# A graph layer on one core: tiles with their own base and 112 columns, last edges' types found by marks, bias kept in PSUM

## Chip, core and metric

The kernel runs on one core of one Trainium2 chip. The metric is the device time of one execution in microseconds (us). Before the change it is 2237.54 us, the median of three runs (2236.86 to 2239.26). Engines are named as the profile names them: PE (TensorE, matmuls) and PEld (its weight loads), DVE (VectorE), ACT (ScalarE), POOL (GpSimd) and SP (SyncE).

## What is computed

The reference is a residual layer of a relational graph network over 12500 nodes with 256 features, 212500 edges sorted by destination, and 8 edge types. Cut to what matters:

```python
h = jnp.maximum(_layernorm(x, axis=-1), 0.0)
hx = jnp.einsum('ni,rio->rno', h, weight)          # 8 types, 256 x 256 each
msg = hx[edge_type, src]
agg = jax.ops.segment_sum(msg, dst, num_segments=12500)
out = x + agg * 0.5**0.5 + h_bias + (h @ loop_weight) * 0.5**0.5
```

Each node has one edge to itself among its edges, and as the sort is stable and these edges were put behind the others, it is the node's last. Some 16 other edges per node come from random pairs.

## The kernel before

**What is added up.** The kernel does not multiply each message by its type's weights. It sums, for each node and type, the rows `h[src]` of that type's edges, transposed, in a ring `acc` (128 features x 2 halves x 8 types x nodes). When all edges of a group of 128 nodes are in, the group's eight sums are multiplied by the eight weight matrices and added in PSUM.

**Units and tiles.** The edges are cut into 796 units of 267 edges in order of destination (`EDGES`). From each unit the last edges of nodes are taken out, by shifting the other edges forward in a packed row (`sources`, `compacted`), and what is left, at most 256 edges, makes two tiles of 128 edges. There are 1592 tiles. Index work is done for blocks of 128 units at a time, one unit per partition (`prepare`, 7 blocks), some 300 tiles ahead and a few operations per tile (`blocks_ahead`, `background`).

**One tile.** `gather` (line 607) is an indirect DMA on POOL that fetches the 128 rows `h[src]`; while `h` is not yet whole in DRAM (the first 96 tiles) it fetches rows of `x`, which `batch` then normalizes in place. Gathers are issued 58 tiles ahead (`AHEAD`), into buffers for 62. `onehots` (line 620) writes, for four tiles at once on DVE, ones where a column's number equals the edge's column (8 types x a node's place). `edge_sums` (line 647) multiplies the two halves of the gathered rows by this. A float matmul shows as two matmuls and two weight loads in the profile, so a tile has four of each. Both tiles of a unit add into one PSUM bank that holds 22 nodes from the unit's base (`WIN`): the first reaches all 22 (176 columns), the second 18 from the fourth on (144 columns, `REACH`). `add_sums` (line 659) then adds these 2 x 8 x 22 sums into the ring on DVE, at an offset that is read from memory into a register (`load_offsets`, sixteen units at a time). The banks for sums are four (`ps_e`), and the add of a unit is issued one unit later (`LAG`).

**One group.** `begin` (lines 671 to 679) transposes the group's own rows of `h` on PE, copies them on ACT, and writes them on DVE into the ring eight times, each time where the node's last edge has that type: this counts the last edges without gathering them. The types come from `find_types` (lines 686 to 706), once for four groups, in the `finish` of the fourth: for each block that holds some of these nodes (34 pairs in all), DVE writes `places` (line 698), ones where a node is the first of a unit, and 22 matmuls of 512 columns each (line 701) spread the types of a unit's first, second, ... last edge to all partitions. `group_work` multiplies the complete sums: for each group a matmul of `one` and `bias_in` (line 752), and 2 x 9 products of sums and weights (line 758). They are dealt out between the following tiles by a budget, and PE's order is thus written out by hand, as is every engine's (`manual_schedule`). `finish` (line 767) adds the product to `x`, three tiles after it is issued (`REST`), and begins the group six further on.

**Order and end.** `Plan` gives for each group the last unit that can touch it (`last`), from a line below which no base lies. A node outside a tile's reach would be counted by `verdict`, and the program's second path (`general_path`) would then run behind the first. On these inputs it does not run.

Of the kernel before, what the change touches and what calls it, by code (L numbers as in the profile page):

```python
# [28 lines left out]
EDGES = 267  # L29


WIN = 22
REACH = ((0, 22), (4, 18))
# [7 lines left out]
AHEAD = 58  # L41

# [25 lines left out]
class Plan:  # L68
# [6 lines left out]
    def __init__(self, N, E):  # L75
        U = EDGES
        self.NU = NU = -(-E // U)
        self.NT = NU * PAIR - (1 if E - (NU - 1) * U <= P else 0)
        slack = 6.5 * (E / 4) ** 0.5 / U + 1.0
        self.rate = rate = E / (N * U)  # L80

        self.low = [(1 / rate, -slack / rate), (1.1 / rate, -(1.5 + 0.1 * E / U) / rate)]
        self.high = [(1 / rate, slack / rate)]
        self.starts = list(range(0, N, GROUP))
        self.ends = self.starts[1:] + [N]
        self.NG = len(self.starts)
        self.last = [
            min([NU - 1, *(int((e + 2 - b) / a) + 1 for a, b in self.low)]) for e in self.ends]
        self.last[-1] = NU - 1

        self.begin = lambda u: max(0.0, *(a * u + b for a, b in self.low))
        self.blocks = [
            [b for b in range(-(-NU // P))
             if self.begin(b * P) <= e + 2
             and self.high[0][0] * min(NU - 1, b * P + P - 1) + self.high[0][1] + 2 * WIN + 2 >= s]
            for s, e in zip(self.starts[::XG], self.starts[XG::XG] + [N])]
        a, b = self.high[0]
        self.first = [max(0, int((s - WIN - 2 - b) / a) - 1) if s else 0 for s in self.starts]

# [101 lines left out]
def kernel(  # L201
# [16 lines left out]
    C = R * max(n for _, n in REACH)  # L218
    assert KC * R * WIN <= 512
# [8 lines left out]
    TB, SB = (R - 1).bit_length(), (WIN - 1).bit_length()  # L228
# [12 lines left out]
    bias_in = const.tile([1, D], F32, name="bias_in")  # L241
    one = const.tile([1, P], F32, name="one")
    w = const.tile([P, KC, R * D], F32, name="w")
    wl = const.tile([P, KC, D], F32, name="wl")
    low = const.tile([P, NB], F32, name="low")
    high = const.tile([P, NB], F32, name="high")
    counts = const.tile([P, NB], F32, name="counts")
    line = const.tile([P, XG * GROUP + WIN - 1], F32, name="line")
# [9 lines left out]
    with ExitStack() as main:  # L258
# [12 lines left out]
        selves = main.enter_context(tc.tile_pool(name="selves", bufs=SLOTS + 1))  # L271
        types = main.enter_context(tc.tile_pool(name="types", bufs=2))
# [8 lines left out]
        ps_o = main.enter_context(tc.tile_pool(name="ps_o", bufs=2, space=PSUM))  # L281
        msg, oh, offsets, kind = {}, {}, {}, {}
        firsts, loops, typed, gidx, col = {}, {}, {}, {}, {}
# [94 lines left out]
        def last_edges(b, got):  # L378
# [24 lines left out]
            def number():  # L403
                got["ends"] = small.tile([P, 1], F32, name="ends")
                nc.vector.tensor_reduce(got["ends"], got["end"], AX.X, ALU.add)

            def kept():
                nc.vector.tensor_single_scalar(
                    work_tile(got, "kinds", 6, I32)[:, :WIN], packed[:, :WIN], 2 * R - 1,
                    op=ALU.bitwise_and)  # L410
                loops[b] = small.tile([P, WIN], BF16, name="loops")
                nc.vector.scalar_tensor_tensor(
                    loops[b], line[:, :WIN], got["ends"], got["kinds"][:, :WIN],
                    op0=ALU.is_lt, op1=ALU.mult)

            return [selves_, ends, moves, codes, packs, number,
                    *compacted(got, TB + 1, (EDGES - 1).bit_length()), kept]

        def columns(b, got):


            halves = [(slice(i * P, (i + 1) * P), o, n) for i, (o, n) in enumerate(REACH)]

            def bases():
                got["base"] = small.tile([P, 1], F32, name="base")
                nc.vector.tensor_scalar(
                    got["base"], firsts[b], low[:, b : b + 1], high[:, b : b + 1],
                    op0=ALU.max, op1=ALU.min)

            def offs():  # L430
                got["off"] = small.tile([P, 1], F32, name="off")
                nc.vector.tensor_tensor(got["off"], firsts[b], got["base"], op=ALU.subtract)
                got["add"] = small.tile([P, PAIR], F32, name="add")
                for i, (_, o, _) in enumerate(halves):
                    nc.vector.tensor_scalar(
                        got["add"][:, i : i + 1], got["off"], float(R), float(1 - R * o),
                        op0=ALU.mult, op1=ALU.add)
# [15 lines left out]
            def moved():  # L453
                work_tile(got, "col", 2)
                for i, (h, _, _) in enumerate(halves):
# [4 lines left out]
            def to():  # L460
                for h, _, n in halves:
                    nc.vector.scalar_tensor_tensor(
                        got["there"][:, h], got["col"][:, h], float(n * R), got["there"][:, h],
                        op0=ALU.is_le, op1=ALU.mult)
# [13 lines left out]
            def all_():  # L478
                nc.vector.scalar_tensor_tensor(
                    got["valid"], got["ends"], float(WIN), got["valid"], op0=ALU.min, op1=ALU.add)  # L480
# [3 lines left out]
            return [bases, offs, fits, number, there, moved, to, final, valid, sum_, all_,  # L484
                    *turned(got, "col", lambda: col.setdefault(b, cols.tile([P, U], F32, name="cols")))]

        def places(b, got):

            def wraps_():
                got["wrapped"] = small.tile([P, NK], F32, name="wrapped")  # L490
                nc.vector.tensor_scalar(
                    got["wrapped"], wraps, got["base"][:, 0:1], None, op0=ALU.is_lt)

            def turns():
                got["turns"] = small.tile([P, 1], F32, name="turns")
                nc.vector.tensor_reduce(got["turns"], got["wrapped"], AX.X, ALU.add)

            def position():
                got["pos"] = small.tile([P, 1], F32, name="pos")
                nc.vector.scalar_tensor_tensor(  # L500
                    got["pos"], got["turns"], float(-RING), got["base"][:, 0:1],
                    op0=ALU.mult, op1=ALU.add)

            def turn():
                pt = ps_d.tile([P, 512], F32, tag="pt", name="ptr")
                nc.tensor.transpose(pt[0:1, :P], got["pos"], ident)
                place[b] = small.tile([1, P], I32, name="offs")
                nc.vector.tensor_copy(place[b], pt[0:1, :P])
# [119 lines left out]
        def load_offsets(u0):  # L628
            n = min(REGS, NU - u0)
            b, q = divmod(u0, P)  # L630
# [3 lines left out]
            for i, v in enumerate(vals):  # L634
                offsets[u0 + i] = v

        def edge_sums(t):
            m, o = msg.pop(t), oh.pop(t)
            if t % PAIR == 0:
                bank = ps_e.tile([P, 512], F32, name="ps")  # L640
                sums["ps"] = bank[:, : KC * R * WIN].rearrange("p (c k) -> p c k", c=KC)
            ps = sums["ps"]
            i = t % PAIR
            from_, width = (a * R for a in REACH[i])
            end = t == NT - 1 or i == PAIR - 1
            for c in range(KC):
                nc.tensor.matmul(  # L647
                    ps[:, c, from_ : from_ + width], m[:, c * P : (c + 1) * P], o[:, :width],
                    start=(i == 0 and c == 0), stop=(end and c == KC - 1))
# [5 lines left out]
        def add_sums(u, ps):  # L655
            a = acc[:, :, :, bass.ds(offsets.pop(u), WIN)]
# [3 lines left out]
            added[u] = i.ins  # L660

            assert all(g in begun for g in range(plan.NG) if plan.first[g] <= u)
# [22 lines left out]

        def find_types(q):

            if XG * q >= plan.NG:
                return
            while any(b not in loops for b in plan.blocks[q]):  # L690
                background.pop(0)[1]()
            d0 = plan.starts[XG * q]
            n = min(N - d0, XG * GROUP)
            bs = plan.blocks[q]
            pt = ps_d.tile([P, 512], F32, tag="pt", name="ptt")
            for b in bs:
                o = types.tile([P, XG * GROUP + WIN - 1], BF16, name="places")
                nc.vector.tensor_scalar(  # L698
                    o, line, firsts[b], float(WIN - 1 - d0), op0=ALU.subtract, op1=ALU.is_equal)
                for k in range(WIN):  # L700
                    nc.tensor.matmul(  # L701
                        pt[:, :n], loops[b][:, k : k + 1].to_broadcast([P, P]),
                        o[:, WIN - 1 - k : WIN - 1 - k + n],
                        start=(b == bs[0] and k == 0), stop=(b == bs[-1] and k == WIN - 1))
            typed[q] = types.tile([P, XG * GROUP], BF16, name="types")
            nc.scalar.activation(typed[q][:, :n], pt[:, :n], AF.Copy)  # L706
# [36 lines left out]
        def group_work(g):  # L743
# [5 lines left out]
            def product(r, c):  # L749
                if (r, c) == (R, 0):  # L750
                    got["out", g] = ps_o.tile([P, D], F32, name="po")
                    nc.tensor.matmul(  # L752
                        got["out", g][:n], one[:, :n], bias_in, start=True, stop=False)
                if r == R:
                    lhs, rhs = got["self", g][:, c, :n], wl[:, c, :]
                else:
                    lhs, rhs = acc[:, c, r, s0 : s0 + n], w[:, c, r * D : (r + 1) * D]
                i = nc.tensor.matmul(got["out", g][:n], lhs, rhs, start=False,  # L758
                                     stop=(r == R - 1 and c == KC - 1))
                if r < R and first_dep[0]:  # L760
# [3 lines left out]
            def finish():  # L764
                q, k = divmod(g, XG)
                rows_ = got["x", q]
                nc.vector.tensor_add(rows_[:n, k, :], rows_[:n, k, :], got["out", g][:n])  # L767
# [9 lines left out]
                if b % XG == XG - 1:  # L777
                    find_types(b // XG + 1)
# [13 lines left out]
        with tc.manual_schedule():  # L792
# [6 lines left out]
            iota_i = ohs.tile([P, XG * GROUP + WIN - 1], I32, tag="oh", name="iota_i")  # L799
            nc.gpsimd.iota(iota_i, pattern=[[1, XG * GROUP + WIN - 1]], base=0, channel_multiplier=0)  # L800
            tid = small.tile([P, NB], I32, name="tid")
            nc.gpsimd.iota(tid, pattern=[[P, NB]], base=0, channel_multiplier=1)
# [4 lines left out]
            nc.vector.memset(one, 1.0)  # L807
# [182 lines left out]
```

## Time and profile before

| | |
|---|---|
| median of the three runs | 2237.54 us |
| profiled execution: its time, its span | 2238.67 us, 2236.7 us |
| PE busy | 1984.4 us, 89% of the span |
| DVE busy | 1290.3 us, 58% |
| POOL busy | 1512.0 us, 68% |
| ACT busy | 170.4 us, 8% |
| mean granted PE clock | 0.94 of full speed |
| edge matmuls (line 647), products (line 758) | 1103.7 us, 981.9 us in both of its groups |
| matmuls for types (line 701), for the bias (line 752) | 210.7 us, 68.6 us |
| gathers (line 607) | 1592, together 1509.7 us |

The span runs from the first to the last instruction on the chip, and the profiled execution's time includes what lies around it. Busy times of matmuls overlap, because each is counted through its way down the array. Rows of the profile read: line, engine, operation, what is written and read, shape, count, then busy time, mean ns of one, and the idle time just before them with what ended it. Rows of the timeline begin with the start and the length in us; a count `x4` means that consecutive instructions of one kind were joined.

### The profile page before, as it was taken

Reading aid. Unit: us, or ns where it says so; the run is one execution under the profiler, and the core shown is the slowest. Engines: PE = TensorE matmul, PEld = TensorE weight load, DVE = VectorE, ACT = ScalarE, POOL = GpSimd, SP = SyncE. Lnnn points to the kernel's source line nnn. Section 1 sums busy time; section 2 is a strip of 40 time slices with the busy share of each in tenths; the row PEclk is TensorE's granted clock in tenths of the full one; section 3 lists DMA queues with packets and bytes.
Section 4 is the critical chain, followed back from the end, with each engine's and each line's share of the span. In section 5 each row is a group of like instructions: output and inputs, shape, how many; then the busy total and the mean of one; then the engine's idle time right before and its main releaser. Section 6 shows DMA issues by size and latency. Waiting matters only on the chain.

```text
span 2236.7 us, 30467 instructions
## 1 busy us (share of the span) xinstructions
PE 1984.4 (89%) x11073; PEld 1699.8 (76%) x11073; DVE 1290.3 (58%) x3124; ACT 170.4 (8%) x373; POOL 1512.0 (68%) x1618
## 2 busy tenths in 40 slices
PE   2236899999999999999999999999999799999999
PEld 1235788787787787797787797787797687897897
DVE  6787754485464485454584454684455475564552
ACT  1465300000000000000000000000000000000000
POOL 6624677676777677776777776777777576777730
PEclk9556999999999999999999999999999899999999
DMA  4785344343344344344343443444344343443420
GB/s 133 227 277 183 90 132 135 96 133 117 110 133 132 99 134 121 113 133 118 114 134 108 125 134 103 135 133 119 115 135 120 94 130 96 134 133 101 129 68 14
DMA packets 145685, 279.14 MB, mean 125 GB/s; under 512 B 27909, under 2 KB 94590, under 8 KB 145534
## 3 DMA queue, kind: packets, MB, share of 16 engines
q0 software_dynamic: 76416, 208.77, 32.3%
q1 hardware_dynamic: 69118, 68.40, 9.6%
q8 instruction: 90, 1.47, 0.3%
q14 instruction: 61, 0.50, 0.1%
HBM read 251.46 MB, written 25.60 MB: 124 GB/s over the span
## 4 chain that ended last, share of the span: by engine, by line
PE 78%; DVE 13%; issue 3%; ACT 2%; POOL 1%; DMA 1%; DVEq 0%; SPq 0%; ACTq 0%; POOLq 0%
PE ps L647 34%; PE po L758 31%; PE ptt L701 9%; DVE acc L679 4%; PE po L752 2%; DVE oh L620 1%; POOL msg L607 1%; DVE acc L659 1%; DVE moves L331 1%; PE pst L671 1%; DVE fixed L332 1%; DVE e_stats L555 1%; DVE n_stats L555 1%; ACT xt L567 1%; ACT self_t L674 0%
## 5 line engine op out<-in xcount | busy, mean ns | idle before, releaser
L607 POOL DMA_INDIRECT msg<-h,gidx x1496 | 1417.4, 947 | 544.8 <-issue 405.9
L647 PE MATMUL ps<-oh,msg 128*128 128x176 f32 (+1 forms) x6368 | 1103.7, 305 | 79.9 <-ACT msg L567 51.7
L647 PEld LDWEIGHTS ps<-oh,msg 128*128 128x128 f32 x6368 | 1028.6, 194 | 154.3 <-ACT msg L567 54.8
L758 PE MATMUL po<-w,acc 128*128 128x256 f32 x3136 | 870.2, 380 | 0.8 <-DVE flag L521 0.8
L620 DVE TENSOR_TENSOR oh<-fixed,cols 128x704 f32<-128x704 f32 x398 | 353.3, 888 | 445.4 <-PE ps L647 439.9
L659 DVE TENSOR_TENSOR acc<-acc,ps 128x352 f32 x796 | 409.3, 514 | 285.4 <-PE ps L647 278.9
L758 PEld LDWEIGHTS po<-w,acc 128*128 128x128 f32 x3136 | 531.8, 190 | 22.8 <-issue 1.0
L679 DVE SCALAR_TENSOR_TENSOR acc<-types,pst 128x256 f32<-128x256 bf16 (+1 forms) x784 | 267.5, 413 | 113.7 <-ACT self_t L674 113.7
L701 PE MATMUL ptt<-places,loops 128*128 128x512 bf16 (+1 forms) x748 | 210.7, 452 | 95.6 <-DVE places L698 94.9
L701 PEld LDWEIGHTS <-loops 128*128 128x128 bf16 x748 | 83.3, 114 | 217.2 <-DVE places L698 99.1
L674 ACT ACTIVATE self_t<-pst 128x256 f32<-128x256 f32 x98 | 37.4, 382 | 1578.5 <-PE pst L671 1578.5
L607 POOL DMA_INDIRECT msg<-in_x_dram,gidx x96 | 92.3, 962 | 94.7 <-issue 60.7
L758 PE MATMUL po<-wl,self_t 128*128 128x256 f32 x392 | 111.7, 408 | 0.0
L758 PEld LDWEIGHTS po<-wl,self_t 128*128 128x128 f32 x392 | 66.7, 190 | 38.2 <-issue 32.9
L752 PE MATMUL po<-bias_in,one 1*128 1x256 f32 x196 | 68.6, 429 | 0.9 <-DVE xr L767 0.9
L567 ACT ACTIVATE xt<-xt,n_shift,n_rstd 128x256 f32<-128x256 f32 x98 | 51.0, 589 | 29.8 <-DVE n_shift L564 29.8
L567 ACT ACTIVATE msg<-msg,e_shift,e_rstd 128x256 f32<-128x256 f32 x96 | 49.8, 589 | 13.4 <-DVE e_shift L564 13.4
L752 PEld LDWEIGHTS po<-bias_in,one 1*128 1x128 f32 x196 | 28.9, 184 | 23.3 <-issue 21.4
L767 DVE TENSOR_TENSOR xr<-xr,po 128x256 f32<-128x256 f32 x98 | 40.3, 412 | 9.1 <-PE po L758 8.7
L331 DVE TENSOR_SCALAR moves<-fixed 128x267 int32<-128x267 int32 x98 | 42.3, 431 | 2.1
L332 DVE COPY_PREDICATED fixed<-moves,fixed 128x266 int32<-128x266 int32 (+6 forms) x98 | 39.3, 401 | 3.4
L706 ACT ACTIVATE types<-ptt 128x512 bf16<-128x512 f32 (+1 forms) x25 | 14.7, 587 | 322.7 <-PE ptt L701 322.7
(92 smaller groups left out, 327.5 us busy)
## 6 DMA issues: line engine op xcount, KB each, us to landing
msg<-h,gidx POOLq DMA_INDIRECT x1496, 2.8
xt<-in_x_dram SPq DMA_DIRECT2D x24, 512.0 KB, 6.2
h<-xt SPq DMA_DIRECT2D x24, 512.0 KB, 3.8
xr<-in_x_dram SPq DMA_DIRECT2D x24, 512.0 KB, 7.7
out_dram<-xr SPq DMA_DIRECT2D x24, 512.0 KB, 3.6
hr<-h SPq DMA_DIRECT2D x23, 512.0 KB, 5.2
w<-in_L_gnn_weight_dram SPq DMA_DIRECT2D x2, 1024.0 KB, 5.9
msg<-in_x_dram,gidx POOLq DMA_INDIRECT x96, 2.9
```

The lines of the kernel that those rows point to most:

```text
L331: nc.vector.tensor_single_scalar(m, packed, 1 << (bit + k), op=ALU.bitwise_and)
L332: nc.vector.copy_predicated(packed[:, : EDGES - (1 << k)], m[:, 1 << k :], packed[:, 1 << k :])
L555: nc.vector.bn_stats(stats[:n, j, :], rows_[j])
L567: nc.scalar.activation(rows_[j], rows_[j], AF.Relu, bias=shift[:n, j : j + 1], scale=rstd[:n, j : j + 1])
L607: nc.gpsimd.indirect_dma_start(out=msg[t], out_offset=None, in_=table[:, :], in_offset=bass.IndirectOffsetOnAxis(ap=gidx[b][:, at : at + 1 ...
L620: nc.vector.tensor_tensor(o[:, k : k + v, :i, :], iota_f.unsqueeze(1).unsqueeze(1).to_broadcast([P, v, i, C]), of.unsqueeze(3).to_broadcas ...
L647: nc.tensor.matmul(ps[:, c, from_ : from_ + width], m[:, c * P : (c + 1) * P], o[:, :width], start=(i == 0 and c == 0), stop=(end and c == ...
L659: i = nc.vector.tensor_tensor(a, a, ps, op=ALU.add)
L679: i = nc.vector.scalar_tensor_tensor(acc[:, :, r, s0 : s0 + n], of, float(r + 1), pst[:, :, :n], op0=ALU.is_equal, op1=ALU.mult)
L701: nc.tensor.matmul(pt[:, :n], loops[b][:, k : k + 1].to_broadcast([P, P]), o[:, WIN - 1 - k : WIN - 1 - k + n], start=(b == bs[0] and k == ...
L752: nc.tensor.matmul(got["out", g][:n], one[:, :n], bias_in, start=True, stop=False)
L758: i = nc.tensor.matmul(got["out", g][:n], lhs, rhs, start=False, stop=(r == R - 1 and c == KC - 1))
```

## The change

Three things are changed together.

1. Each tile has its own base, its own 14 nodes (112 columns) and its own add into the ring. The base of a unit's second tile is the node of its 129th remaining edge. Both tiles' sums lie beside each other in one bank. Adds, offsets, `Plan.last` and `Plan.first` count tiles instead of units.
2. Types of last edges: per block and per four groups DVE writes two rows of marks over the 512 nodes, one from each unit's first node on and one from its end on (`mark`, one group earlier than the rest). Products of 24 columns of these marks with the unit's 22 types and its first node, and with the same numbers negated, give each node, on its own partition, its unit's types and first node. DVE picks the node's own type, ACT writes it on a diagonal, and one matmul of 512 columns with ones spreads it to all partitions, three tiles later (`spread_types`).
3. The bias is copied once into the second half of the two output banks, and DVE adds it to `x` in `finish`; the matmul with `one` is gone.

```diff
-WIN = 22
-REACH = ((0, 22), (4, 18))
+LASTS = 22
+WIN = 14
...
         def edge_sums(t):
...
-            ps = sums["ps"]
-            i = t % PAIR
-            from_, width = (a * R for a in REACH[i])
-            end = t == NT - 1 or i == PAIR - 1
+            ps = sums["ps"][:, t % PAIR]
             for c in range(KC):
-                nc.tensor.matmul(
-                    ps[:, c, from_ : from_ + width], m[:, c * P : (c + 1) * P], o[:, :width],
-                    start=(i == 0 and c == 0), stop=(end and c == KC - 1))
+                nc.tensor.matmul(ps[:, c], m[:, c * P : (c + 1) * P], o, start=True, stop=True)
...
+        def mark(q):
...
+                for i, edge in enumerate((firsts[b], stops[b])):
+                    nc.vector.tensor_scalar(
+                        m[:, i, :], line, edge, float(-plan.starts[XG * q]),
+                        op0=ALU.subtract, op1=ALU.is_ge)
...
         def find_types(q):
...
-                for k in range(WIN):
+            parts = [(b, m, i) for b, m in marked.pop(q) for i in range(2)]
+            for g in range(XG):
+                for b, m, i in parts:
                     nc.tensor.matmul(
-                        pt[:, :n], loops[b][:, k : k + 1].to_broadcast([P, P]),
-                        o[:, WIN - 1 - k : WIN - 1 - k + n],
-                        start=(b == bs[0] and k == 0), stop=(b == bs[-1] and k == WIN - 1))
+                        pt[:, g, :], m[:, i, g * GROUP : (g + 1) * GROUP], loops[b][:, i, :],
+                        start=(b, m, i) == parts[0], stop=(b, m, i) == parts[-1])
...
+            nc.vector.tensor_tensor(one, one, pt[:, :, :LASTS], op=ALU.mult)
+            kinds = small.tile([P, XG], F32, name="kinds")
+            nc.vector.tensor_reduce(kinds, one, AX.X, ALU.add)
+            marked[q] = marks.tile([P, XG * GROUP], BF16, name="diagonal")
+            for g in range(XG):
+                nc.scalar.activation(
+                    marked[q][:, g * GROUP : (g + 1) * GROUP], ident, AF.Copy,
+                    scale=kinds[:, g : g + 1])
+
+        def spread_types(q):
+
+            pt = ps_d.tile([P, 512], F32, tag="pt", name="ptt")
+            nc.tensor.matmul(pt, ones_b, marked.pop(q), start=True, stop=True)
             typed[q] = types.tile([P, XG * GROUP], BF16, name="types")
-            nc.scalar.activation(typed[q][:, :n], pt[:, :n], AF.Copy)
+            nc.scalar.activation(typed[q], pt, AF.Copy)
...
             def finish():
                 q, k = divmod(g, XG)
                 rows_ = got["x", q]
+                nc.vector.tensor_add(rows_[:n, k, :], rows_[:n, k, :], outs[g % 2][:n, 1, :])
                 nc.vector.tensor_add(rows_[:n, k, :], rows_[:n, k, :], got["out", g][:n])
...
+                if b % XG == XG - 2 and XG * q < plan.NG:
+                    mark(q)
+                if b % XG == XG - 1 and XG * q < plan.NG:
+                    find_types(q)
+                    done["late"].append((done["tile"] + REST, lambda: spread_types(q)))
...
-                if t % PAIR == PAIR - 1 or t == NT - 1:
-                    waiting.append((t // PAIR, ps))
-                while waiting and (len(waiting) > LAG or t == NT - 1):
-                    u, ps = waiting.pop(0)
-                    add_sums(u, ps)
+                waiting.append((t, ps))
+                while waiting and (
+                        t == NT - 1 or t % PAIR == PAIR - 1 and len(waiting) > LAG * PAIR):
+                    for i in range(min(PAIR, len(waiting))):
+                        u, ps = waiting.pop(0)
+                        add_sums(u, ps)
```

## The prediction

> **What bounds the kernel now.** I read the page's busy shares first, then its groups of part 5, then GpSimd's gathers in windows, the timeline of a steady stretch around 1200 us, the groups kept apart by shape, the list of waits, and the timeline of the end.
>
> ```profile
> PE 1984.4 (89%) x11073; PEld 1699.8 (76%) x11073; DVE 1290.3 (58%) x3124; ACT 170.4 (8%) x373; POOL 1512.0 (68%) x1618
> ```
>
> By these busy times TensorE looks like the bound, and GpSimd (POOL) seems to have a third of its time free. It has not:
>
> ```profile
> 1200.63 0.65 PE L647 MATMUL ps<-oh,msg 128*128 128x144 f32 x4
> ...
> 1201.55 0.76 PE L647 MATMUL ps<-oh,msg 128*128 128x176 f32 x4
> 1201.66 0.95 POOL L607 DMA_INDIRECT msg<-h,gidx  x1 [0.30 <-issue]
> ...
> 1202.92 0.94 POOL L607 DMA_INDIRECT msg<-h,gidx  x1 [0.30 <-issue]
> ...
> 1204.10 1.03 PE L758 MATMUL po<-w,acc 128*128 128x256 f32 x4
> ```
>
> Gathers start 1.25 us apart: 0.95 us of work and 0.30 us of "issue", in which GpSimd waits for nothing that the profile shows. The same 1.25 us stands between the first gathers at 13 us, when nothing holds them. So one gather per tile, 1592 of them, costs 1990 us of a span of 2236.7 us. The windows of line 607 show how near it is:
>
> ```profile
> 0.00:300.00 300.00, 160.58 (x169) 0.74 0.59 182
> 300.00:2153.00 1853.00, 1349.16 (x1424) 0.97 0.41 121
> ```
>
> 169 gathers have started by 300 us, the other 1423 take until 2152.2 us: 1.302 us each. TensorE's tiles go at the same pace (the windows of line 647 count 5848 matmuls, four a tile, from 250 to 2150 us: 1462 tiles, 1.30 us each). TensorE sets it: a gather can run only 58 to 62 tiles ahead, and 103.9 us of GpSimd's waits end with a matmul of line 647. When the gathers stop, TensorE still has 84.5 us of work:
>
> ```profile
> 2222.58 0.65 PE L647 MATMUL ps<-oh,msg 128*128 128x144 f32 x4
> ...
> 2232.80 0.42 DVE L767 TENSOR_TENSOR xr<-xr,po 84x256 f32<-84x256 f32 x1 [8.35 <-PE po L758]
> ```
>
> So TensorE is the bound by only 0.05 us a tile; GpSimd comes next.
>
> **The change, TensorE.** Edge sums: each of a tile's four matmuls gets 112 columns instead of 176 or 144.
>
> ```profile
> L647 PE MATMUL ps<-oh,msg 128*128 128x176 f32 x3184 | 622.9, 319 | 79.9 <-ACT msg L567 51.7 <-DVE n_rstd L563 16.9 <-issue 10.0
> L647 PE MATMUL ps<-oh,msg 128*128 128x144 f32 x3184 | 531.1, 290 | 0.0
> ...
> L758 PEld LDWEIGHTS po<-w,acc 128*128 128x128 f32 x3104 | 526.9, 190 | 20.8 <-issue 1.0
> ...
> L758 PEld LDWEIGHTS po<-w,acc 128*84 128x84 f32 x32 | 4.9, 153 | 2.0
> ```
>
> A duration includes the way through the array, so I take spacings: four 176s in 0.76 us with 319 ns for the last are (760-319)/3 = 147 ns apart, four 144s 120 ns, both 0.83 ns a column. 112 columns would be 93 ns. But a weight load grows by 37 ns for 44 columns (190 against 153), 0.84 ns each, so 128 columns hold it for 108 ns. I take 108, the later of the two (bounds 93 and today's mean 133.5): 6368 x 25.5 ns = 162 us less (0 to 258).
>
> Types of last edges: 748 matmuls go, at (4930-452)/21 = 213 ns (the 22 at 1948.40 us on the chain took 4.93 us): 159 us, and with them the wait before each batch, since the places are written behind a group's eight updates on VectorE:
>
> ```profile
> PE ptt L701 <- DVE places L698: 94.9, 24, 8.5
> ```
>
> In their place each of 25 batches gets about 11 products of 24 columns (68 pairs of block and mark, times 4 groups, over 25), at most 114 ns each (bf16 weight load of line 701), one of 512 columns (0.45 us), and a wait for ScalarE's four diagonals, priced by today's waits between nothing and 3.7 us; I take 1.5. That is 3.2 us x 25 = 80 us (43 to 135). Its marks are written a group earlier, so nothing stands before the small products. Net 174 us less (119 to 211).
>
> Bias: 196 matmuls at 0.69-0.43 = 0.26 us, 51 us less. Together 387 us (170 to 520), 0.24 us a tile: TensorE's own pace falls from 1.30 to 1.06 us (0.97 to 1.19). Even the slow end is under 1.25.
>
> **VectorE.** Two rows give its price per element:
>
> ```profile
> L620 DVE TENSOR_TENSOR oh<-fixed,cols 128x704 f32<-128x704 f32 x398 | 353.3, 888 | 445.4 <-PE ps L647 439.9
> L659 DVE TENSOR_TENSOR acc<-acc,ps 128x352 f32 x796 | 409.3, 514 | 285.4 <-PE ps L647 278.9
> ```
>
> The one-hots have 352 elements more than the adds and take 374 ns more: 1.06 ns each and 140 ns fixed. An add of 224 elements is 378 ns, and there are 1592 for 796: +193 us. A one-hot of 448 is 616 ns: -108. Bias adds 98 x 0.41: +40. Marks 68 x 0.49 against 34 places: +17. Six small operations a batch, some 1.2 us x 25: +30. Fifty more loads of sixteen offsets, 0.64 us of idle behind the one at 1157 us: +32. Longer preparation of 7 blocks, about 2 us each: +14. In all +218 us, 0.14 a tile. From 250 to 2150 us VectorE is busy 1070.6 us, 0.73 a tile; it comes to 0.87, under 1.25 if its waits don't grow. While a block is prepared it is over 1.25 for some 48 tiles, which the 62 tiles of messages cover.
>
> **The sum.** Both are quicker than a gather, so GpSimd stops waiting and TensorE catches up until it waits for messages. From 300 us: 1423 x 1.25 = 1779, so the last gather ends at 2079. The start: TensorE has up to 27 us less to do there (113 tiles), VectorE up to 15 us more, and they alternate: 0 (-27 to +15). Marks beside gathers: 34 places delayed them by about 1.5 us in all (one of 2.12 us at 32 us, one of 1.18 at 318): +3 for twice as many (0 to 34). So 2082. Then the tail: landing 1.9 us (2.8 from issue, 0.95 of it work); products that wait behind the last tiles, since group 96 is complete only four tiles before the end and a tile leaves TensorE some 0.8 us: 6 us (0 to 16); last tile 0.65, its two adds 0.8, the last group's 36 products 8, bias and output adds 0.8, the last store 3.5 as now (2236.7-2233.2). That is 21.6 against 84.5 now, so the span is 2103.6. The profiled execution took 2238.67, 1.97 more than its span, and the median shown, 2237.54, is 1.13 under that: **2105 us**.
>
> **A rule weighed.** Of all rows beside a place marker, gathers show 942 to 964 ns nearly everywhere, and 2117 once. The Trainium skill, "SBUF — State Buffer", section "Who interferes with whom", says that a VectorE instruction in a two-port mode keeps GpSimd fully out of their shared ports for its length, and that this form can enter such a mode: a rule against this change, which has twice as many of them. By it 68 x 0.5 us would be lost and the time be 2136; the row gives 3 us, and I keep the row.
>
> **Rivals.**
> *The pair stays the bound (0.12).* TensorE and VectorE wait for each other tile by tile, and their joint pace stays between 1.27 and 1.31: 300 + 1423 x 1.29 = 2136, and behind the last gather stand some 45 us, half of today's 84.5: 2135 to 2230, 2180 in the middle. For it: VectorE's waits today,
>
> ```profile
> DVE oh L620 <- PE ps L647: 439.9, 262, 13.7
> ...
> DVE acc L659 <- PE ps L647: 278.9, 208, 14.2
> ```
>
> Against it: these are waits for a TensorE that is slow.
> *VectorE becomes the bound, slower (0.08).* Its adds stand in order behind the wait for each tile's sums, and there are now twice as many. If every add kept the 0.35 us that it waits now (278.9/796), that is 279 us more beside 1508 busy and 719 of today's waits: 2506 at the worst, 2367 with half of the extra. It decides from 1.31 us a tile, 0.44 over the 0.87. The gathers' lead and the sums' four banks speak against it.
> *It doesn't do what it says (0.01).* An edge outside the 14 nodes sends the whole run to the general path, thousands of us. On the inputs drawn the widest tile spans 12.
> *The start gains too (0.04).* GpSimd loses 300-13-211 = 76 us before 300 us; if a third goes with the shorter matmuls, 2055 to 2078.
> *Gathers are the bound (0.75).* 2078 to 2135, the forecast.
>
> Range: the forecast's cases from 2076, and the quicker half of the pair's: 2076 to 2165. The rest, 0.19, is left out. A measurement of this kernel tells about 0.2% (4.5 us) from no change: faster 0.90, within it 0.02, slower 0.08.
>
> **What would show it.** Right: gathers 1.25 us apart without a break from 300 us to about 2080; TensorE idle with messages as the releaser; edge matmuls near 108 ns apart; adds near 0.38 us, one-hots near 0.62; no wait of 3.7 us before the types; some 22 us from the last gather to the end. Wrong: gathers still waiting for line 647's matmuls after 400 us, VectorE above 85% busy, a gather's own time above 1 us, or a start later than now by more than 15 us.

## The result and the profile after

The changed kernel takes 2130.33 us (median of 4 runs, 2122.65 to 2131.13) against 2237.20 us for the kernel before, run beside it (4 runs, 2236.08 to 2239.26). The ratio is 0.9514, with a 95% interval of 0.9491 to 0.9537: faster, as predicted, and inside the range, but 25 us above the point of 2105. The profiled execution took 2129.83 us with a span of 2128.1. The last four experiments ran on another chip, on which the kernel before took 2779.33 us; their times can't be set beside the others, and why that chip is slower is not settled.

The busy times, from the page of the kernel after:

```profile
PE 1642.2 (77%) x10433; PEld 1497.1 (70%) x10433; DVE 1475.9 (69%) x4268; ACT 202.5 (10%) x473; POOL 1515.6 (71%) x1619
```

No engine is now above 77%. Read by this row alone, nothing bounds the kernel. The gathers' windows (line 637 of the kernel after; columns: stretch, its length, GpSimd's busy time and count of gathers in it, TensorE's granted clock, share of DMA time, GB/s) show what stands closest to it:

```profile
0.00:300.00 300.00, 160.45 (x168) 0.78 0.59 182
300.00:2100.00 1800.00, 1352.79 (x1424) 0.91 0.42 124
2100.00:2128.20 28.20, 0.00 (x0) 0.97 0.10 31
```

By 300 us 168 gathers have run (before: 169), and the other 1424 end at 2099.1 us: 1.263 us each instead of 1.302. The profiled execution is 108.8 us shorter, and nearly all of that lies in two places. The last gather ends 53 us earlier (2099.1 for 2152.2), and the tail behind it is 29.0 us instead of 84.5, which is 55.5 us less. The start gave nothing.

The groups of the parts that changed, from the page's part 5 (busy and mean of one; then the idle time before them and what ended most of it):

```profile
L637 POOL DMA_INDIRECT msg<-h,gidx x1496 | 1421.1, 950 | 489.6 <-issue 413.9
L674 PE MATMUL ps<-oh,msg 128*128 128x112 f32 x6368 | 961.2, 283 | 272.3 <-issue 96.3
L684 DVE TENSOR_TENSOR acc<-acc,ps 128x224 f32 x1592 | 613.1, 385 | 122.6 <-PE ps L674 77.3
L650 DVE TENSOR_TENSOR oh<-fixed,cols 128x448 f32<-128x448 f32 x398 | 246.8, 620 | 204.5 <-PE ps L674 173.0
```

TensorE now idles 272.3 us ahead of the edge matmuls, and what GpSimd waits for between gathers is mostly the "issue" of 0.30 us again (time in which the profile shows nothing that it waits for). VectorE's waits for TensorE, 439.9 and 278.9 us before, are 173.0 and 77.3: the adds stand closer behind TensorE although there are twice as many.

Three rows of the list of waits are new or were expected to go (engine, what it was about to write and its line, what ended the wait; total, times, longest):

```profile
DVE gidx L326 <- DMA msg<-h,gidx: 101.1, 4, 33.8
PE ptt L731 <- DVE acc L704: 83.6, 23, 7.0
DVE rise L348 <- DMA nat_d<-in_dst_dram: 79.7, 3, 71.2
```

The last one hides the largest loss, a single wait of 71.2 us. The timeline of GpSimd, VectorE and TensorE around 1714 us shows where it comes from:

```profile
1713.26 0.95 POOL L637 DMA_INDIRECT msg<-h,gidx  x1 [0.30 <-issue]
1714.22 0.37 POOL L306 IOTA nat_d<- 128x268 int32 x1
1714.61 0.27 SPq L311 DMA_DIRECT2D nat_d<-in_dst_dram  x1
...
1716.46 0.44 DVE L348 TENSOR_TENSOR rise<-nat_d 128x267 f32<-128x267 int32 x1 [71.17 <-DMA nat_d<-in_dst_dram]
...
1718.64 1.60 PE L674 MATMUL ps<-oh,msg 128*128 128x112 f32 x6 [68.19 <-DVE acc L684]
```

The last block of edges is not full, so its index tile is first filled with padding by an iota on GpSimd (line 306), and only then loaded. The iota takes 0.37 us. But it stands in GpSimd's queue behind all the gathers issued ahead of it, and comes up at 1714.22. VectorE has been waiting for the loaded block since 1645.29, its adds stand behind that wait, and TensorE, without free banks for its sums, stands still for 68.19 us. The releaser that the profile names is the load; the cause is the iota ahead of it, as e4 below shows. The windows of all engines (PE, PEld, DVE, ACT, POOL busy, then the clock) show both halves of the loss:

```profile
1600.00:1700.00 100.00, 46.60 (x283) 41.14 (x281) 30.63 (x81) 0.77 (x2) 75.63 (x81) 0.73 0.41 122
1700.00:1800.00 100.00, 64.43 (x373) 58.39 (x374) 69.25 (x201) 3.41 (x9) 66.60 (x71) 0.76 0.38 109
```

In the first, TensorE is busy for 46.6 us, all but a trace of it before 1650, while the gathers go on (81 instructions of GpSimd in 100 us). In the second the gathers have filled all the message buffers and must wait in turn: 71. Between 1700 and 1800 us their starts lie 13.3 us further apart, in all, than 1.25 us each.

### The profile page after: what moved, and what is told of

It reads as the page before. It is cut to its first block, busy times and chain, and to the rows that moved or that the text cites. A ratio compares the mean times of both kernels' runs of the same rounds, so it can differ in the third digit from the quotient of the medians.

```text
span 2128.1 us, 31245 instructions
## 1 busy us (share of the span) xinstructions
PE 1642.2 (77%) x10433; PEld 1497.1 (70%) x10433; DVE 1475.9 (69%) x4268; ACT 202.5 (10%) x473; POOL 1515.6 (71%) x1619
## 4 chain that ended last, share of the span: by engine, by line
PE 62%; DVE 17%; issue 10%; POOL 4%; DMA 3%; ACT 2%; DVEq 1%; SPq 0%; ACTq 0%; POOLq 0%
PE po L808 33%; PE ps L674 28%; DVE acc L704 5%; POOL msg L637 4%; DVE acc L684 3%; DMA msg<-h,gidx 2%; DVE moves L338 1%; DVE e_stats L585 1%; ACT xt L597 1%; PE pst L696 1%; DVE fixed L339 1%; DVE n_stats L585 1%; DVE oh L650 1%; ACT self_t L699 1%; PE ptt L731 1%
## 5 line engine op out<-in xcount | busy, mean ns | idle before, releaser
L674 PEld LDWEIGHTS ps<-oh,msg 128*128 128x128 f32 x6368 | 960.3, 201 | 372.1 <-issue 179.9
L674 PE MATMUL ps<-oh,msg 128*128 128x112 f32 x6368 | 961.2, 283 | 272.3 <-issue 96.3
L808 PE MATMUL po<-w,acc 128*128 128x256 f32 x3136 | 922.8, 398 | 0.8 <-DVE flag L551 0.8
L684 DVE TENSOR_TENSOR acc<-acc,ps 128x224 f32 x1592 | 613.1, 385 | 122.6 <-PE ps L674 77.3
L650 DVE TENSOR_TENSOR oh<-fixed,cols 128x448 f32<-128x448 f32 x398 | 246.8, 620 | 204.5 <-PE ps L674 173.0
L808 PEld LDWEIGHTS po<-wl,self_t 128*128 128x128 f32 x392 | 75.4, 214 | 7.4
L731 PE MATMUL ptt<-loops,mark 128*128 128x24 bf16 x272 | 11.4, 178 | 85.8 <-DVE acc L704 83.6
L731 PEld LDWEIGHTS <-mark 128*128 128x128 bf16 x272 | 9.0, 100 | 95.2 <-DVE acc L704 89.2
L326 DVE CAST gidx<-ptr 128x256 int32<-128x256 f32 x7 | 2.9, 420 | 103.5 <-DMA msg<-h,gidx 101.1
L696 PE MATMUL pst<-ident,hr 128*128 128x128 f32 (+1 forms) x184 | 35.9, 278 | 35.4 <-DVE gidx L326 33.9
L696 PEld LDWEIGHTS pst<-ident,hr 128*128 128x128 f32 (+1 forms) x184 | 23.6, 151 | 35.8 <-DVE gidx L326 34.0
```

What stands on the lines that cost most here:

```text
L650: nc.vector.tensor_tensor(o[:, k : k + v, :i, :], iota_f.unsqueeze(1).unsqueeze(1).to_broadcast([P, v, i, C]), of.unsqueeze(3).to_broadcas ...
L674: nc.tensor.matmul(ps[:, c], m[:, c * P : (c + 1) * P], o, start=True, stop=True)
L684: i = nc.vector.tensor_tensor(a, a, ps, op=ALU.add)
L696: nc.tensor.transpose(pst[:, c, :n], rows_[:n, c * P : (c + 1) * P], ident[:n, :n])
L731: nc.tensor.matmul(pt[:, g, :], m[:, i, g * GROUP : (g + 1) * GROUP], loops[b][:, i, :], start=(b, m, i) == parts[0], stop=(b, m, i) == pa ...
L808: i = nc.tensor.matmul(got["out", g][:n], lhs, rhs, start=(r == R and c == 0), stop=(r == R - 1 and c == KC - 1))
```

## The experiments

**Theories.** *Gathers:* after the change the gathers' period of 1.25 us is the bound, and the gap to the forecast is the iota's wait. *The pair (rival):* TensorE and VectorE, which hand tiles to each other, are still the bound or close to it, and less work for them gives more time. A second question is which of the three parts (tiles of 112 columns, types, bias) brought the gain.

### One more instruction behind each gather

e1_extra_after and e2_extra_before put a GpSimd memset of one column behind each gather, in the kernel after and in the kernel before:

```diff
+    spare = const.tile([P, 1], F32, name="spare")
...
+            nc.gpsimd.memset(spare, 0.0)
```

> The changed kernel with one more instruction on GpSimd behind each gather, a memset of one column of a tile that nothing reads. Seventeen such memsets took 0.63 us at the start of the kernel before, 37 ns each. Theory (gathers set the pace after the change): every ns that a gather's period grows is paid 1592 times, so at least 1592 x 0.037 = 59 us more, about 2190 us, and the growth is 1592 times the growth of the period that the trace shows. Rival (TensorE and VectorE as a pair set the pace, GpSimd has 29% idle): at most 10 us more, 2130 to 2140.

> The kernel before with the same memset behind each gather. Theory (TensorE set the pace at 1.30 us a tile, a gather's period of 1.25 has 0.05 us to spare): if the period grows by 37 ns nothing is lost, 2237 to 2247 us; if it grows by more than 0.05 us, only what is over is paid, and the loss is some 80 us less than in the changed kernel. Rival (gathers bound the kernel before as well): the same loss as in the changed kernel, 59 us or more.

Measured: 2138.82 us (ratio to the kernel before 0.9569, 0.9546 to 0.9593) and 2237.51 us (1.0014, 1.0001 to 1.0026). The kernel after lost 8.5 us, not the expected 59. GpSimd's timeline in the first shows why:

```profile
599.88 0.95 POOL L638 DMA_INDIRECT msg<-h,gidx  x1 [0.19 <-issue]
600.82 0.12 POOL L641 MEMSET spare<- 128x1 f32 x1
601.13 0.95 POOL L638 DMA_INDIRECT msg<-h,gidx  x1 [0.19 <-issue]
```

The period is still 1.25 us: the memset takes 0.12 us, not the expected 37 ns, out of the gap of 0.30, and 0.19 is left. The 8.5 us come from thirteen intervals of 2.42 us: the last gather ends 15.3 us later (2114.4), and the tail behind it is 23.3 us instead of 29.0. What makes these intervals is not known. The experiment does not tell the theories apart, since the load it was to put on the gathers did not arrive. It shows that the gap has room for another short instruction.

The load was made larger, a memset of 256 columns (e9_long_extra_after, e10_long_extra_before), on the slower chip:

```diff
-    spare = const.tile([P, 1], F32, name="spare")
+    spare = const.tile([P, 256], F32, name="spare")
```

> The changed kernel with a memset of 256 columns behind each gather. The one of a single column took 0.12 us and fitted into the 0.30 us between gathers, so the period stayed 1.25 us. One of 128 columns took 0.21 us at the start of the kernel before, so 256 take some 0.33, and the period grows by 0.03 to 0.22 us. Theory (gathers set the pace): the time grows by 1500 to 1592 times the growth of the period that the trace shows, between 45 and 350 us. Rival (the pair of TensorE and VectorE, at about 1.2 us a tile): nothing is lost up to some 0.05 us.

> The kernel before with the memset of 256 columns behind each gather. Theory (TensorE set the pace at 1.30 us, with 0.05 us to spare): the loss is 0.05 x 1423 = 74 us smaller than that of the changed kernel with the same memset, or smaller still by TensorE's end of 84.5 us that hides behind the slower gathers; both kernels come within 60 us of each other, since both then go at the gathers' pace. Rival (no shared bound): they stay 107 us apart.

```profile
1500.70 0.95 POOL L638 DMA_INDIRECT msg<-h,gidx  x1 [0.17 <-issue]
1501.66 0.33 POOL L641 MEMSET spare<- 128x256 f32 x1
1502.15 0.95 POOL L638 DMA_INDIRECT msg<-h,gidx  x1 [0.17 <-issue]
```

These lines are from e9. Now the period grows, to 1.45 us in 1468 of its intervals: 0.95, 0.33 and 0.17. That is the memset and not the chip: in e12, on the same chip without it, 1267 intervals lie within 5 ns of 1.25 us. The time is 2470.72 us, 340 us above the 2130 of the kernel after on another chip; 1592 x 0.20 is 318. These numbers lie close, but they are no evidence for the gathers as the bound. In e9 TensorE does not catch up with them: from 400 us to the last gather (at 2394.4 us) 31 to 62 messages lie ready whenever it begins a tile, it waits for messages 0.1 us in all, and the tail behind the last gather is 74.8 us. The kernel before with the same memset took 2553.24 us, less than the 2779.33 it takes without it on that chip; why is not known. The two runs with the memset lie 82.5 us apart, between the 60 us at most of the theory and the 107 of the rival. The pair of runs does not settle what the bound is.

### Less work for the pair

e3_96_columns makes the tiles 96 columns wide instead of 112. It leaves VectorE 1394.9 us of work instead of 1475.9, and TensorE shorter matmuls:

```diff
-WIN = 14
+WIN = 12
```

> The changed kernel with 12 nodes (96 columns) for a tile instead of 14, which is as wide as the widest tile of these inputs. Theory (gathers): nothing but a few us at the start and the end, 2118 to 2131 us. Rival (the pair sets the pace): VectorE saves 32 elements an add and 16 columns of a one-hot at 1.06 ns, 0.05 us a tile or 81 us, TensorE up to 0.05 us a tile: 2050 to 2090.

Measured: 2120.87 us (0.9491, 0.9472 to 0.951), 9.5 us quicker than the kernel after, inside what the gathers' theory gives and far above the 2050 to 2090 of the rival. 81 us less for VectorE bring under 10.

e11_half_the_gathers asks the opposite: how quick is the pair when gathers cost half? The second tile of each unit uses the first one's rows, so the sums are not the layer's; the work on them is the same, and half of the gathers are left out (padding and preparation as in e8 below):

```diff
+            if i:
+                msg[t] = msg[t - 1]
+                return
```

> The changed kernel with early padding and preparation 240 ahead, in which only the first tile of each unit is gathered and the second multiplies the same rows again: half of the gathers are left out, all other work stays. It measures the pace of TensorE and VectorE without the gathers' bound. Theory (TensorE at 1.06 us a tile after the change, with a start of 300 us to tile 117 that the gathers hardly set, and 13 us at the end): 300 + 1475 x 1.06 + 13 = 1877 us. Rival (VectorE, with its own waits, is as slow as the gathers): 2060 to 2111.

Measured: 1956.4 us (1953.08 to 1959.59), on the slower chip. GpSimd now waits for TensorE, 932.0 us in all, and TensorE's edge matmuls in the window of its line from 500 to 1500 us give the pair's own pace:

```profile
500.00:1500.00 1000.00, 532.58 (x3616) 537.32 (x3614) 0.94 0.29 84
```

3616 matmuls are 904 tiles: 1.106 us each, with whatever that chip costs included. That is under a gather's 1.25, so the rival falls, as far as the pair goes as quickly beside all gathers as beside half of them, which this run does not show; e8, below, has all of them. The time lies 79 us above the theory's 1877 and 104 below the rival's 2060, so the pair has some 0.14 us a tile to spare, not 0.2 (more, if the chip's stops are in the 1.106).

### The padding made early

e4_pad_early makes the padding once, at the start, and lets VectorE copy it, so that nothing but gathers stands in GpSimd's queue. e8_pad_prep also begins the preparation of a block later, 240 tiles ahead of its use instead of 300:

```diff
-                        nc.gpsimd.iota(
-                            n, pattern=[[2, EDGES + 1]], base=N - 2 * EU, channel_multiplier=0)
+                        nc.vector.tensor_copy(n, pad)
...
+            nc.gpsimd.iota(
+                pad, pattern=[[2, EDGES + 1]], base=N - 2 * EU, channel_multiplier=0)
```

```diff
-PREP = 300
+PREP = 240
```

> The changed kernel, in which the padding of the last block's destinations is counted out by GpSimd at the start, into a tile of its own, and copied by VectorE when the block is prepared; before, GpSimd did it in the middle of the gathers. Theory (the instruction stands in GpSimd's queue behind 58 gathers that are issued ahead but not yet run, so VectorE waits 71 us for it at 1645 us, TensorE stands still and gathers stop for 13 us, and TensorE ends 8 tiles behind): no wait of 71 us, no stop of the gathers, 13 to 20 us less, 2110 to 2118 us. Rival (the messages' buffers cover that wait): 2126 to 2131.

> The changed kernel with the early padding and with a block's preparation begun 240 tiles ahead instead of 300. Theory (at 300 VectorE waits 33 us in three of the blocks for the last gathers of the block two before, whose indices it overwrites, since TensorE has caught up with the gathers; at 240 these gathers are done): the waits of VectorE's index write on gathers (101 us) go, but the gathers never stood still for them, so the time is that with the early padding alone, within 5 us. Rival (these waits are paid in the end): some 30 to 100 us less than with the padding alone.

Measured: 2111.89 us (0.9452, 0.9433 to 0.9472) and 2110.89 us (0.9439, 0.9412 to 0.9466). The iota is what caused the 71 us wait, and that cost the kernel 18 us. The windows of the gathers' line in e4:

```profile
0.00:300.00 300.00, 159.63 (x168) 0.78 0.59 182
300.00:2088.00 1788.00, 1353.61 (x1425) 0.92 0.43 125
2088.00:2111.00 23.00, 0.00 (x0) 0.99 0.13 39
```

The gathers end at 2087.4 us, 11.7 earlier; the tail is 23.0 instead of 29.0. Over 300 us to the end their starts lie only 6.8 us further apart than 1.25 each (19.2 in the kernel after).

e4 also tells what the new wait at the index write is worth. VectorE's wait at line 326 grew to 132.3 us, and the time still fell. There are two buffers of indices, so block b overwrites those of block b-2. When gathers run only some tiles ahead of TensorE, a preparation that begins 300 tiles early comes to this write before the last gathers of block b-2 have run. In e8 that wait is gone and the time is the same within 1 us; instead TensorE waits for messages, as it should behind a bound of gathers (in 466 of the 1379 tiles that it begins between 400 us and the last gather, at most three lie ready; in the kernel before it never had fewer than 49):

```profile
PE ps L674 <- DMA msg<-h,gidx: 79.7, 129, 3.3
POOL msg L637 <- PE ps L674: 60.6, 188, 2.1
```

```profile
1000.31 0.67 PE L674 MATMUL ps<-oh,msg 128*128 128x112 f32 x4 [0.62 <-DMA msg<-h,gidx]
...
1001.21 0.94 POOL L637 DMA_INDIRECT msg<-h,gidx  x1 [0.30 <-issue]
1001.48 0.70 PE L674 MATMUL ps<-oh,msg 128*128 128x112 f32 x4 [0.50 <-DMA msg<-h,gidx]
```

(Waits, then the timeline, of e8.) Together with e4, whose runs overlap with its runs, this is the quickest kernel with all gathers, 5.6% below the one before and 0.9% below the one after.

### The parts by themselves

e5_only_tiles has the new tiles with the old types and the old bias; e6_only_types has the new types in the kernel before, with two message buffers fewer for the room; e7_old_bias takes only the bias back out of the kernel after:

```diff
# e5
-            m = marks.tile([P, 2, XG * GROUP], BF16, tag=f"mark{k}", name="mark")
+                o = types.tile([P, XG * GROUP + LASTS - 1], BF16, name="places")
...
# e6
-MSGS = 62
-AHEAD = 58
+MSGS = 60
+AHEAD = 56
...
# e5 and e7
+                    i = nc.tensor.matmul(
+                        got["out", g][:n], one[:, :n], bias_in, start=True, stop=False)
...
-                nc.vector.tensor_add(rows_[:n, k, :], rows_[:n, k, :], outs[g % 2][:n, 1, :])
```

> Only the first part of the change: own bases and 112 columns; the types by 22 large matmuls and the bias by a matmul as before. Theory (TensorE at 1.30 - 0.10 = 1.20 us a tile is quicker than a gather's 1.25, and that is enough): nearly the whole gain, 2120 to 2165 us. Rival (the three parts add up by TensorE's work that they take away, 162 of 387 us): 2237 - 0.42 x 107 = 2192.

> Only the second part: the types by marks, in the kernel before (units of 22 nodes, bias by a matmul), with messages for 60 tiles and gathers 56 ahead instead of 62 and 58, since the memory doesn't hold both. Theory (TensorE at 1.30 - 0.11 = 1.19 us a tile, under a gather's 1.25): nearly the whole gain, 2110 to 2150 us. Rival (shares of TensorE's work, 174 of 387 us): 2237 - 0.45 x 107 = 2189.

> The changed kernel with the bias by a matmul again and no bias add on VectorE. Theory (gathers): 196 matmuls more on TensorE (51 us) and 98 adds less on VectorE (40 us) move nothing but the catching up at the end, 2125 to 2140 us. Rival (the pair): 20 to 50 us, one way or the other.

Measured: 2168.85 us (0.9703, 0.9675 to 0.9731), 2163.01 us (0.9669, 0.9639 to 0.97) and 2143.38 us (0.9587, 0.956 to 0.9614). All three end a little above what the gathers' theory gave (by 4, 13 and 3 us), e5 and e6 below the rival's 2192 and 2189, and e7 under the 20 us from which the rival counted. The windows of the edge matmuls, of e5 and then of e6, show TensorE's pace while it still had a lead of messages:

```profile
500.00:1100.00 600.00, 280.81 (x1959) 283.76 (x1959) 0.97 0.43 124
```

```profile
500.00:1100.00 600.00, 346.71 (x2007) 324.51 (x2006) 0.96 0.44 128
```

1959 matmuls are 490 tiles in 600 us, 1.225 us each; 2007 are 502, 1.196. Either part alone brings TensorE from 1.30 under 1.25, and with that the last gather comes earlier: 2107.9 (e5), 2090.7 (e6) and 2096.0 us (e7), against 2099.1 with all parts and 2152.2 before. What remains differs mostly behind the last gather. The tails are 58.3, 71.0 and 43.0 us, for 29.0 with all parts and 84.5 before. At 300 us TensorE stands some 50 tiles behind the gathers, and it gains slowly: at 1600 us 20 (e5), 25 (e6) and 15 tiles (e7) are left. Then the padding of the last block takes the gain back, as in the kernel after (waits of e5, e6 and e7):

```profile
DVE rise L349 <- DMA nat_d<-in_dst_dram: 60.0, 3, 50.9
DVE rise L344 <- DMA nat_d<-in_dst_dram: 56.3, 3, 48.4
DVE rise L349 <- DMA nat_d<-in_dst_dram: 76.8, 3, 67.6
```

Behind these single waits of 50.9, 48.4 and 67.6 us TensorE stands still for 48.1, 43.0 and 65.4 us, and at 1800 us it is 57, 51 and 54 tiles behind again, with 300 us of gathers left to catch up. So a large part of the tails is this stop, and no run shows what each part would bring without it. As the kernels stand, the tiles alone bring 69 us, the types alone 75, and all three parts together 107: the first part past the gathers' pace gets most of the gain, and the others mainly shorten the tail. Taking the bias back out costs 13 us: the gathers end 3 us earlier, and the tail is 14 us longer.

### Both reserves together

e12_best joins e8 with 96 columns and uses the room for two more message buffers, on the slower chip:

```diff
-WIN = 14
+WIN = 12
...
-MSGS = 62
-AHEAD = 58
+MSGS = 64
+AHEAD = 60
```

> The changed kernel with early padding, preparation 240 ahead, 96 columns, and messages for 64 tiles with gathers 60 ahead. Theory (gathers): two more gathers run while the start holds them, 2.5 us, and the 96 columns give some 5 us at the start and the end: 2100 to 2109 us. Rival (nothing left but the gathers' 1990 us and a start that none of this shortens): 2109 to 2113.

Measured: 2586.99 us, against 2779.33 for the kernel before on that chip. Nothing follows for the expectation of 2100 to 2109. The timeline shows stops on TensorE for which no releaser is seen:

```profile
919.55 0.59 PE L674 MATMUL ps<-oh,msg 128*128 128x96 f32 x4 [0.29 <-issue]
920.99 0.24 PE L674 MATMUL ps<-oh,msg 128*128 128x96 f32 x1 [0.85 <-issue]
921.71 0.24 PE L674 MATMUL ps<-oh,msg 128*128 128x96 f32 x1 [0.47 <-issue]
923.11 0.48 PE L674 MATMUL ps<-oh,msg 128*128 128x96 f32 x3 [1.16 <-issue]
```

There are 222 such stops ahead of line 674, 179.5 us in all, some of them between matmuls of one tile, whose message is there already. Whether e12 would beat e8 on the other chips stays open.

## Why the prediction was right, and where it was off

**The bound: right.** It named the gathers' period, not the busiest engine, as what comes next, and that both partners would be quicker. The period is 1.25 us in 1470 of 1591 intervals, 168 gathers had run by 300 us where 169 did before ("the start: 0"), and a gather's mean is 950 ns. One of its signs did not come as written: in the kernel after TensorE waits only 14.1 us for messages, since four stops of 30.0, 33.9, 31.6 and 68.2 us, behind the index writes and the padding, each gave the gathers a new lead. With these stops gone, in e8, the waits for messages are there.

**"1423 x 1.25 = 1779, so the last gather ends at 2079": 17 us short with the marks' 3 us counted (2082 for 2099.1).** This is the step that failed. It held only gathers in GpSimd's queue. It overlooked the iota of the last block. The trace of before has it too, as a wait of VectorE of 9.98 us, which the prediction did not take up:

```profile
1761.57 0.44 DVE L341 TENSOR_TENSOR rise<-nat_d 128x267 f32<-128x267 int32 x1 [9.98 <-DMA nat_d<-in_dst_dram]
```

What made it dear is the change itself. The iota stands in GpSimd's order 58 gathers ahead of TensorE's tile. Before, nearly all of those 58 had been run by the time TensorE was there, and 49 to 62 tiles of messages lay ready; now TensorE has caught up (5 tiles behind at 1600 us), the 58 are still to be run, 58 x 1.25 = 72 us, and there is hardly a lead to live on meanwhile. The stop of the gathers that follows is 13.3 of the 17 us. Without it, in e4, the last gather ends at 2087.4 for 2082.

**The tail, 21.6 us predicted, 29.0 measured.** (The prediction's own terms add up to 2104.4; it gives 2105.) The part after the last tile was right: from its end at 2115.1 us to the end of the span are 13.0 us, predicted 13.1 (0.8 for the adds, 8 for the products, 0.8, 3.5).

```profile
2098.20 0.94 POOL L637 DMA_INDIRECT msg<-h,gidx  x1 [0.30 <-issue]
...
2114.50 0.59 PE L674 MATMUL ps<-oh,msg 128*128 128x112 f32 x4
...
2115.99 7.14 PE L808 MATMUL po<-w,acc 128*84 128x256 f32 x32
...
2123.62 0.42 DVE L820 TENSOR_TENSOR xr<-xr,po 84x256 f32<-84x256 f32 x1
```

The last tile ends 16.0 us behind the last gather, not 8.6: TensorE is still eight tiles behind at 2100 us, a remainder of the same stop: without it, in e4, the tail is 23.0.

**TensorE: about right.** Four edge matmuls were to be 108 ns apart. Sixteen in one group of the timeline give (1930 - 283)/15 = 110:

```profile
690.45 1.93 PE L674 MATMUL ps<-oh,msg 128*128 128x112 f32 x16
```

The pace of 1.06 us a tile held while there was a lead (378 matmuls from 300 to 400 us are 94.5 tiles, 1.06 us each); e11 measured 1.106 for the pair over a longer stretch.

**"Nothing stands before the small products": wrong, and without cost.** TensorE waits as before ahead of each batch, 83.6 us for 94.9:

```profile
673.82 1.08 DVE L704 SCALAR_TENSOR_TENSOR acc<-types,pst 128x256 f32<-128x256 bf16 x3
...
674.96 0.56 PE L731 MATMUL ptt<-loops,mark 128*128 128x24 bf16 x16 [3.31 <-DVE acc L704]
```

The marks are indeed written early. But the products write a PSUM bank which the eight updates of the group before (line 704) read, and wait for these. I had attributed the old wait to the places alone. The diagonals on ScalarE, taken at 1.5 us a batch, cost TensorE 7.0 us in all, in two waits. Sixteen of the products themselves take 0.56 us.

**VectorE: 1508 us predicted, 1475.9 measured.** Adds were put at 378 ns and took 385, one-hots at 616 and took 620, and the small operations came to the 30 us that were predicted. The difference is one term: the 32 us for more loads of offsets were read from idle time (0.64 us behind one load), and are not busy time of VectorE.

**The rule on the ports.** The marks are 68 with a mean of 496 ns, and 37 gathers overlap one. These gathers have a median of 1.02 us instead of 0.95, and lengthen by 4.8 us in all. The prediction's 3 us had the size. The Trainium skill, "SBUF — State Buffer", section "Who interferes with whom", says that, with VectorE in a two-port mode, whichever of it and GpSimd issues first gets the shared ports for its whole instruction and fully blocks the other. The direction fits in part: 21 of the 37 gathers beside a mark took over 1.0 us, but 16 did not, and 23 other gathers over 1.0 us stand beside no mark. The estimate of 34 us, with GpSimd locked out for the whole of each mark, would have been seven times too much.

**The wait at the index write (101.1 us) was not foreseen.** e4 and e8 show that it cost nothing that can be told: without the stop at the padding, the time is 2112 with it and 2111 without.

**The rivals.** The pair as the bound is refuted by e3, by the waits for messages in e8 and, with half of the gathers, by e11. VectorE as the bound needed 1.31 us a tile; in e11 the pair, VectorE included, runs at 1.106. The quicker start did not come.

## What to carry to other kernels

When a change lifts the bound, look for the next one by period (start to start), not by busy share: GpSimd at 68% busy was 96% taken (1.25 of 1.302 us). Then ask of each queue with work issued far ahead what else stands in it: here an instruction of 0.37 us waited behind the whole lead of gathers, and that did harm just when the consumer had caught up. And where a second bound stands close behind the first, parts need not add: here two of the three, each alone, brought most of the gain, and what the others brought was found at the end of the kernel.

## What the runs showed of the hardware

- Between two indirect gathers GpSimd shows no work for 0.30 us, and a memset of 0.12 us fits into it without lengthening the period (1.25 us, e1); one of 0.33 us lengthens it to 1.45 (e9).
- The 37 gathers beside a mark (496 ns on VectorE) took 1.02 us in the median, for 0.95 us of all gathers.
- Where TensorE waits, its granted clock is lower: from 1650 to 1700 us of the kernel after, in which it is busy for 0.4 us, the clock is 0.52, and in the 50 us ahead of that 0.93. Over the whole span the mean fell from 0.940 before to 0.892 after, with 461 us at the low clock instead of 272. What that costs was not measured.
- The same kernel (before) took 2237 us on the other chips and 2779 us on one. In e12, which ran on that one, TensorE stood still ahead of its edge matmuls for up to 6.7 us at a time with no releaser in the trace. The cause is open.
